# Layer 1's attention in pairs of units: two projections in one piece, end steps at even units, one fill, and a few orders in the tail

## The chip, the core and the metric

The kernel runs on one core of a Trainium2 chip. The core has five engines with a queue of instructions each: TensorE (PE, with its weight loads shown as PEld), VectorE (DVE), ScalarE (ACT), GpSimd (POOL) and SyncE (SP, which here only issues transfers). Each runs its own instructions in order and waits on semaphores for the others. The metric is the device time of one execution in microseconds (us); lower is better.

## The reference

Two transformer layers on x of shape (8, 256, 128), in fp32. Both modulate a layer norm with values from a small conditioning matrix, add attention, modulate a second layer norm, and add a mixture of experts. Layer 0 has 16 heads of 8 and eight GELU experts with a shared one, top 2. Layer 1, where nearly all of the change is, has 16 heads of 64 and 16 gated experts of width 64 with a shared one, also top 2:

```python
def _L1_attn_ref(x, w_q, w_k, w_v, w_o):
    q = jnp.einsum('bsd,hqd->bhsq', x, w_q)
    k = jnp.einsum('bsd,hqd->bhsq', x, w_k)
    v = jnp.einsum('bsd,hvd->bhsv', x, w_v)
    scores = jnp.einsum('bhsq,bhtq->bhst', q, k)
    masked = jnp.where(causal, -jnp.inf, scores)
    weights = jax.nn.softmax(masked / jnp.sqrt(jnp.float32(dq)), axis=-1)
    out = jnp.einsum('bhst,bhtv->bhsv', weights, v)
    return jnp.einsum('bsf,df->bsd', out.transpose(0, 2, 1, 3).reshape(b, s, -1), w_o)

def _L1_ffn_ref(x, ...):
    router_logits = jax.nn.sigmoid(x @ gate_w + gate_b)
    expert_values, expert_indices = jax.lax.top_k(router_logits, k=2)
    expert_values = expert_values / jnp.sum(expert_values, axis=-1, keepdims=True)
    ...   # silu(x Wg) * (x Wu) Wd of each expert, the two chosen ones weighted
    return x + _mlp(x, shared_wg, shared_wu, shared_wd) + expert_weighted

x = L0_attn_x
...   # layer 0 in the same form
h = _layernorm(x, axis=-1) * (1 + ca) + sa
x = x + ga * _L1_attn_ref(h, ...)
h = _layernorm(x, axis=-1) * (1 + cb) + sb
x = x + gb * _L1_ffn_ref(h, ...)
```

## The kernel before, in words

The kernel does layer 0's attention first, then layer 0's experts in tiles of 128 rows gathered by expert, then a loop over layer 1's attention, then a tail with layer 1's experts. Every engine's instructions are laid out in the order in which the program emits them; there is no planner.

**The loop.** Layer 1's attention has 32 units n (N, L2040): batch b = n // 4, and four heads each (u = n % 4). A unit consists of scores (`scores1`, L1666: 16 matmuls, Exp on ACT, the causal mask on POOL, L822), the projections of q and k (`project_qk1`, L1639) and of v (`project_v1`, L1651), and the values with the sums of the weights (`values1`, L1687). The result of q goes from PSUM to SBUF on DVE (L1649), those of k and v on ACT. The projections run two units ahead: in unit n the program emits scores(n), q and k of n + 2, values(n − 1), v of n + 2. Besides these there are three tables of steps hung on units: `at_head` (behind a given head's mask in the scores), `at` (behind q and k, "early") and `at_end`. Into them go the rest of layer 0 and what prepares layer 1's experts:

- the gathers (L1063, POOL) and sums (`combine`) of layer 0's expert outputs for a later batch, and the layer norm (`first_norm`: measure, normalise, modulate);
- when a batch is through, its reciprocals (`reciprocals1`, L1712, with two transfers rd and rb on SP's queue and `judge`, L817 and L818, on DVE), the four products with rb (`normalise1`, L1729), the output projection (`finish1`, L1745);
- the second layer norm of a span of batches (`norm1`), and its route (`route1`, L1790), a generator that is advanced a step at a time by `go`: logits, the sigmoid, the top two, weights, ranks (`place_steps`, L903), and then indirect scatters of the tokens into xs (L935, POOL), four for each batch;
- `clear` (L889), two fills of xs with zeros at the first units of batches 2 and 3; scatters wait for both.

**PSUM.** The tag "p" (`ps_ln`) has two buffers of one bank each, used in turn by q, k and v projections, the output projection y, transposes, logits and ranks. "s" has two buffers of two banks, for scores and the gated hidden layers; "o" and "sum" have one buffer each.

**The tail.** Ten tiles of four expert blocks (turn1, hidden1, project_tiles) run between the last norms, the routes of batches 6 and 7 (go6, go7) and the table steps (`tables`, L1017 to L1036) that find for each token where its expert's rows went. Then POOL issues 24 indirect gathers (`gather1`, L1063) with a small memset ahead of each (`apart_on_gpsimd`, L1407), which fetch the expert outputs of batches 0 to 5. Beside them run the shared expert (`shared_hidden`, `shared_project`) and, for batches 6 and 7, all 16 experts densely (`dense_hidden`, L1945), weighted by rows of gates (`gate_rows`, L1919). `combine1`, `dense_project` and `ffn1_add` end the kernel.

Of the kernel before, what the change touches and what calls it, by code (L numbers as in the profile page):

```python
# [16 lines left out]
P = 128  # L17
# [540 lines left out]
def fast_path(ctx: ExitStack, tc: tile.TileContext, i: dict, out: bass.AP, bad: bass.AP):  # L558
# [302 lines left out]
    class Sorted:  # L861


        def __init__(self, pool, tag, ne, nt, nd):
            self.pool, self.tag, self.ne, self.nt, self.nd = pool, tag, ne, nt, nd
            self.cap = cap = nt * P
            self.placed = 0
            self.fills, self.scatters = [], []
            f32 = lambda shape, name: pool.tile(shape, F32, name=f"{name}{tag}")
            self.s12 = f32([P, nt, 2, ne], "s12")  # L870
            self.slot = f32([P, nt, 2], "slot")
            self.region = f32([P, ne], "region")

            self.seen = pool.tile([P, nt + 1, ne], BF16, name=f"seen{tag}")
            self.yidx = pool.tile([P, nt, 2], I32, name=f"yidx{tag}")
            self.rowi = pool.tile([P, nd], I32, name=f"rowi{tag}")
            self.widx = pool.tile([P, nd], I32, name=f"widx{tag}")
            self.xs = dram.tile([ne * cap, P], F32, name=f"xs{tag}")
            self.ys = dram.tile([(ne + nd) * P, P], F32, name=f"ys{tag}")
            nc.gpsimd.tensor_scalar(self.region, num[:, :ne], float(cap), 0.0, ALU.mult, ALU.add)  # L880
            nc.gpsimd.memset(self.seen[:, 0, :], 0.0)
            self.marks = [pool.tile([P, 7, ne], BF16, name=f"marks{tag}{n}") for n in range(E1 // ne)]
            for t in self.marks:
                nc.gpsimd.memset(t[:, 0:3, :], 0.0)
# [1 line left out]
        def tmp(self, shape, name, dt=F32, bufs=2):  # L886
            return self.pool.tile(shape, dt, tag=name, bufs=bufs, name=f"{name}{self.tag}_{self.n}")

        def clear(self, zero, part=0, parts=1):  # L889
            m = zero.shape[1]  # L890
            n = self.ne * self.cap // m // parts
            rows = self.xs.rearrange("(p a) c -> p (a c)", p=P).rearrange("p (n m) -> p n m", m=m)
            self.fills.append(
                nc.sync.dma_start(
                    out=rows[:, bass.ts(part, n), :], in_=zero.unsqueeze(1).to_broadcast([P, n, m])
                ).ins
            )

        def place(self, *args):
            for _ in self.place_steps(*args):  # L900
# [39 lines left out]
        def apart(self, ins):  # L940


            group = f"scatters{self.tag}"
            if self.scatters:
                tc.declare_no_dep(ins, group=group, reason="different rows")
                for fill in self.fills:
                    tc.add_manual_dep(ins, fill.name, WAIT, reason="rows are cleared first")
            tc.add_to_no_dep_group(group, ins)
            self.scatters.append(ins)

# [105 lines left out]
                in_offset=bass.IndirectOffsetOnAxis(ap=self.widx[:, d : d + 1], axis=0),  # L1056
            )

        def gather(self, yg, j, between=lambda: None):

            for k in range(2):
                between()
                nc.gpsimd.indirect_dma_start(  # L1063
                    out=yg[:, k, :], out_offset=None, in_=self.ys[:, :],
                    in_offset=bass.IndirectOffsetOnAxis(ap=self.yidx[:, j, k : k + 1], axis=0),
                )
# [400 lines left out]
    at_end(18, first_gates)  # L1467
    at_end(20, first_gates)
    norm6, norm7 = norm0(SPANS0[4]), norm0(SPANS0[5])
    at_end(21, lambda: turn_gates0(0))  # L1470
    at_end(22, lambda: turn_gates0(1))
    at_end(23, norm6[0], lambda: ways[SPANS0[3]]())

    project0(0)
    project_v0(0)
# [314 lines left out]
    def route1(bs):  # L1790


        nt = 2 * bs[1]
        t = bass.ds(2 * bs[0], nt)
        name = f"1_{bs[0]}"
        shape = [P, nt, E1]
        lg = ps_ln(shape, f"lg{name}")
        for j in range(nt):
            c = bass.ts(2 * (bs[0] % 2) + j, P)
            nc.tensor.matmul(out=lg[:, j, :], lhsT=h[bs[0] // 2][:, c], rhs=w1["gate_w"], start=True, stop=True)  # L1800
        p = lp.tile(shape, F32, tag="pr", name=f"p{name}")
        nc.vector.tensor_tensor(p, lg, gate_b.unsqueeze(1).to_broadcast(shape), ALU.add)
        if bs[0] < B - 2:
            nc.scalar.activation(p, p, AF.Exp, scale=-1.0)
        else:
            nc.gpsimd.tensor_tensor(p, one_by_e.unsqueeze(1).to_broadcast(shape), p, ALU.pow)
        yield

        nc.vector.tensor_scalar(p, p, 1.0, None, ALU.add)
        nc.vector.reciprocal(p, p)  # L1810
        sparse = bs[0] < 2 * LAST
        part = bass.ds(2 * (bs[0] % 2), nt)
        s = z1.s12[:, t] if sparse else last12[:, part]
        g = g12_1[:, t]
        yield from top2_steps(lp, p, s, g, name)
        yield
        red = lp.tile([P, nt, 1], F32, tag="red", name=f"red{name}")
        nc.vector.tensor_tensor(red, g[:, :, 0:1], g[:, :, 1:2], ALU.add)
        nc.vector.reciprocal(red, red)
        nc.vector.tensor_tensor(g, g, red.to_broadcast([P, nt, 2]), ALU.mult)  # L1820
        if sparse:
            yield
            yield from z1.place_steps(2 * bs[0], nt, lambda: tokens1[bs], ps_ln)
        else:
            nc.vector.tensor_tensor(s, s, g.unsqueeze(3).to_broadcast([P, nt, 2, E1]), ALU.mult)
            nc.vector.tensor_tensor(gates1[:, part], s[:, :, 0, :], s[:, :, 1, :], ALU.add)
# [91 lines left out]

    def gate_rows(k):  # L1919

        gT_ps = pp.tile([E1, 2, P], F32, tag="s", name=f"gT1_{k}")
        for j in range(2):
            nc.tensor.transpose(gT_ps[:, j, :], gates1[:, 2 * k + j, :], ident)
        gT = lp.tile([E1, 2, P], F32, tag="yg", bufs=3, name=f"gTs1_{k}")
# [80 lines left out]
    def gather1(j):  # L2005
        k, n = divmod(j, 3)
        if n == 0:
            sums["yg", k] = lp.tile([P, 3, 2, P], F32, tag="pt", bufs=4, name=f"yg1_{k}")
        z1.gather(sums["yg", k][:, n], j, apart_on_gpsimd)

    def weigh1(w):

# [16 lines left out]
    def flag():  # L2029
# [1 line left out]
        whole = small.tile([P, 1], F32, tag="whole", bufs=1, name="whole")  # L2031
        nc.vector.tensor_reduce(whole, good, AX.X, ALU.min)
        yield
        cnt = pp.tile([1, 1], F32, tag="s", name="good_cnt")
        nc.tensor.matmul(out=cnt, lhsT=whole, rhs=nums[:, 1:2], start=True, stop=True)
        nc.vector.tensor_scalar(bad, cnt, most[0:1, :], 1.0, ALU.is_lt, ALU.mult)

# [21 lines left out]
    at(1, normalise)  # L2059
    at_end(1, modulate)  # L2060
    for j in range(2):
        at_head(0, 1 + 2 * j, lambda j=j: gather(2, j))
        at_head(1, 1 + 2 * j, lambda j=j: gather(3, j))
    at_end(1, lambda: combine(2))
    at_end(2, lambda: combine(3))
    for w in range(1, NW):
        n = 8 * w
        if w > 1:
            for k in range(4):
                at_head(n - 13 + k, 3, lambda w=w, k=k: gather(2 * w + k // 2, k % 2))  # L2070
            at_end(n - 9, lambda w=w: combine(2 * w))
            at_end(n - 8, lambda w=w: combine(2 * w + 1))
        measure, normalise, modulate = first_norm(w)
        n -= 7 if w > 1 else 6
        at_end(n, measure)
        at(n + 1, normalise)
        at_end(n + 1, modulate)
    for b in range(B - 1):
        n = 4 * b + 6 if b < B - 2 else N - 1
        at(n, *[lambda b=b, u=u: normalise1(b, u) for u in range(4)])  # L2080
        at_end(n, lambda b=b: finish1(b))
    for bs in ((0, 2), (2, 2), (4, 1), (5, 1)):
        n = 4 * sum(bs) + 2
        measure, normalise, modulate, tokens, add = norm1(bs)
        go = one(route1(bs))
        at_end(n, measure)
        at(n + 1, normalise)
        at_end(n + 1, modulate, tokens)
        at(n + 2, go)
        at_end(n + 2, go, go, go, go)  # L2090
        if bs[0] < 5:
            at(n + 4, go)
        else:
            at_end(n + 3, go)
        for k in range(4 * bs[1]):
            if bs[0] < 5:
                at_head(n + 5 + k // 2, 1 + 2 * (k % 2), go)
            else:
                at_head(n + 4, k, go)
        if bs[0] < 5:  # L2100
            at_end(n + 7, add)
    tables = one(z1.tables_steps(ps_ln, True))
    at_end(29, tables, lambda: fetch_weights1(4), lambda: fetch_weights1(5))
    at_end(30, *[lambda m=m: fetch_rows1(m) for m in range(4)], *[lambda m=m: find_rows1(m) for m in range(4, NQ)],
          lambda: fetch_weights1(6))

    for n in range(N):
        b, u = divmod(n, 4)
        scores1(b, u, behind.pop(n, {}))
        if n == 0:  # L2110
            nc.gpsimd.memset(sel, 0.0)
            nc.gpsimd.affine_select(
                out=sel, in_=sel, compare_op=ALU.not_equal, fill=1.0, base=0,
                pattern=[[-8, 4], [-32, 2], [-64, 2], [0, D1]], channel_multiplier=1,
            )
        if n + 2 < N:
            project_qk1(*divmod(n + 2, 4))
        for step in early.pop(n, ()):
            step()
        if n:  # L2120
            values1(*divmod(n - 1, 4))
        if n + 2 < N:
            project_v1(*divmod(n + 2, 4))
        if u == 0 and b:
            reciprocals1(b - 1)
            if b in (2, 3):
                z1.clear(zero1, b - 2, 2)
        for step in ends.pop(n, ()):
            step()


    norms = [norm1((b, 1)) for b in (B - 2, B - 1)]
# [13 lines left out]
    fetch_weights1(8)  # L2146
    hidden1(2)
    turn1(4)
    for _ in range(3):
        tables()  # L2150
    hidden1(3)
    norms[0][0]()
    project_tiles(2)
    hidden1(4)
    turn1(5)
    norms[0][1]()
# [4 lines left out]
    project_tiles(4)  # L2161
    spread_last((2, 3))
    hidden1(5)
    go6()
    finish1(B - 1)
    turn1(7)
# [34 lines left out]
    judge(st1["r", B - 1])  # L2201
    judged = flag()
    next(judged)
    shared_project(2)
    weigh1(2)
    dense_hidden(0)
    gate_rows(1)
    dense_hidden(1)
    dense_hidden(2)
    next(judged, None)  # L2210
    dense_hidden(3)
    dense_gate(0)
    dense_hidden(4)
# [125 lines left out]
```

## Time and profile before

| what | us |
|---|---|
| median of 14 runs (lowest, highest) | 608.98 (603.65, 613.98) |
| the profiled execution | 610.83 |
| its span | 609.0 |
| layer 1's attention loop, 240.20 to 491.00 | 250.80 |
| its PE busy time | 243.14 |
| routed tiles, 491 to 540 | 49 |
| 24 gathers issued, 540 to 575 | 35 |
| end, 575 to 609 | 34 |

Times in the views are microseconds from the span's start. A busy share is the part of the span in which an engine was at work; "<-" behind a group names what ended the idle time before it, "remote" a signal whose sender the profile does not resolve. The chain is followed back from the last instruction, and "issue" in it is time in which the engine waited for nothing that the profile shows. The granted clock is the part of TensorE's full speed that it was given. Unit 12 starts at 337.95 in the trace, unit 13 at 344.68; a unit without anything besides its own work takes 6.73.

### The profile page before, as it was taken

To read this page: it belongs to the slowest core of one execution; us is meant where nothing else is said; L and a number is where in the kernel's file an instruction comes from. 1 tells how busy PE (TensorE), PEld (TensorE's weight loads), DVE (VectorE), ACT (ScalarE), POOL (GpSimd) and SP (SyncE) were. 2 spreads that over 40 slices of the span, in tenths; PEclk is the share of its full clock that TensorE was granted. 3 is DMA by queue.
4 is the path that set the end of the run, shared out by engine and by line. 5 is a ranking of instruction groups with operands and counts; after the bars stand their busy time and mean duration, and the time that the engine had idled before them with its cause. 6 is when DMAs were issued, how large, how long until landed. Compare 5 with 4: busy or idle time off the path is not lost.

```text
span 609.0 us, 12026 instructions
## 1 busy us (share of the span) xinstructions
PE 543.8 (89%) x4499; PEld 385.3 (63%) x4499; DVE 325.3 (53%) x988; ACT 262.7 (43%) x492; POOL 272.8 (45%) x425
## 2 busy tenths in 40 slices
PE   5999998989999998999999998999989898960694
PEld 4355553468999986667667675767667576830264
DVE  4258885556322224764465646565574957660153
ACT  3677774244555533553345333443525421250110
POOL 5324676474444123854124508331654530788300
PEclk9999998799999999999999999999989998996687
DMA  8699100315999614104086593012030366552401
GB/s 273 252 398 407 38 20 30 126 41 171 318 353 351 215 40 156 32 18 93 1 258 236 131 380 93 13 26 47 19 86 14 86 199 171 155 132 56 97 19 56
DMA packets 53582, 85.40 MB, mean 140 GB/s; under 512 B 6668, under 2 KB 32780, under 8 KB 52364
## 3 DMA queue, kind: packets, MB, share of 16 engines
q1 hardware_dynamic: 45324, 60.50, 31.2%
q0 software_dynamic: 8048, 23.67, 11.9%
q8 instruction: 37, 0.61, 0.4%
q10 hardware_dynamic: 144, 0.39, 0.2%
q14 instruction: 29, 0.24, 0.1%
HBM read 53.46 MB, written 31.07 MB: 139 GB/s over the span
## 4 chain that ended last, share of the span: by engine, by line
PE 68%; DVE 11%; DMA 6%; issue 6%; ACT 4%; POOL 3%; SPq 0%; POOLq 0%; ACTq 0%; DVEq 0%
PE sc L1676 6%; PE hp L1356 6%; PE yt L1364 6%; PE sc L1125 5%; PE o L1698 5%; PE qp L1645 5%; DMA xs<-zero 4%; PE vp L1658 4%; PE kp L1645 4%; PE y L1751 4%; PE o L1159 3%; PE gud L1948 3%; PE sum L1706 3%; PE qk L1089 2%; PE sc L1137 1%
## 5 line engine op out<-in xcount | busy, mean ns | idle before, releaser
L822 POOL TENSOR_SCALAR_AFFINE_SELECT pt<-pt 128x256 f32<-128x256 f32 (+1 forms) x144 | 67.5, 496 | 146.0 <-ACT pt L1679 111.4
L1063 POOL DMA_INDIRECT yg<-ys,yidx x56 | 54.2, 968 | 32.8 <-DMA ys<-ysb 20.5
L1679 ACT ACTIVATE pt<-sc 128x768 f32<-128x768 f32 x64 | 48.4, 808 | 26.1 <-PE sc L1676 25.7
L1141 ACT ACTIVATE pt<-sc 128x1024 f32<-128x1024 f32 x48 | 46.7, 1026 | 26.0 <-PE sc L1125 14.7
L1676 PEld LDWEIGHTS sc<-q,k 64*128 64x128 f32 x512 | 41.6, 187 | 18.8 <-issue 13.9
L1698 PE MATMUL o<-pt,v 128*64 128x256 f32 (+1 forms) x512 | 50.4, 337 | 2.9 <-POOL pt L822 1.8
L1676 PE MATMUL sc<-q,k 64*128 64x256 f32 (+1 forms) x512 | 50.5, 337 | 0.0
L1358 ACT ACTIVATE hst<-hp,wt 128x128 f32<-128x128 f32 x136 | 38.8, 368 | 25.8 <-ACT hst L1358 24.2
L1661 ACT COPY v<-vp 128x512 f32<-128x512 f32 x32 | 18.7, 585 | 70.5 <-PE vp L1658 70.5
L1698 PEld LDWEIGHTS o<-pt,v 128*64 128x64 f32 x512 | 32.8, 139 | 20.8 <-POOL pt L822 7.9
L1054 POOL DMA_INDIRECT wt<-in_wpk_dram,widx x31 | 29.5, 950 | 33.8 <-PE xT L1347 27.9
L1649 DVE COPY q<-qp 128x512 f32<-128x512 f32 x32 | 22.0, 688 | 36.4 <-PE qp L1645 36.3
L1645 PE MATMUL qp<-h,wq 128*128 128x256 f32 x128 | 36.0, 404 | 3.6 <-DVE q L1649 2.3
L1369 DVE COPY ysb<-yt 128x128 f32<-128x128 f32 x39 | 11.4, 292 | 49.8 <-PE yt L1364 49.8
L935 POOL DMA_INDIRECT xs<-ht0b,idx x32 | 31.9, 996 | 11.0 <-issue 8.0
L1125 PE MATMUL sc<-qm,k 32*128 32x512 f32 x192 | 35.0, 722 | 1.6 <-ACT pt L1141 1.0
L1658 PE MATMUL vp<-wv,h 128*128 128x512 f32 x64 | 36.0, 645 | 0.0
L1356 PE MATMUL hp<-xTs,wt 128*128 128x128 f32 x272 | 35.9, 275 | 0.0
L1364 PE MATMUL yt<-wt,hst 128*128 128x128 f32 x272 | 35.8, 275 | 0.0
L1645 PE MATMUL kp<-h,wk 128*128 128x256 f32 x128 | 33.6, 386 | 0.0
L1649 ACT COPY k<-kp 128x512 f32<-128x512 f32 x32 | 18.8, 587 | 33.5 <-PE kp L1645 33.5
L1356 PEld LDWEIGHTS hp<-xTs,wt 128*128 128x128 f32 x272 | 33.0, 192 | 0.0
(306 smaller groups left out, 1095.1 us busy)
## 6 DMA issues: line engine op xcount, KB each, us to landing
xs<-zero SPq DMA_DIRECT2D x2, 6144.0 KB
xs<-zero SPq DMA_DIRECT2D x1, 8192.0 KB
rb<-rd SPq DMA_DIRECT2D x14, 512.0 KB
mdb<-mrd SPq DMA_DIRECT2D x2, 2048.0 KB
xg<-xs SPq DMA_DIRECT2D x63, 64.0 KB
wt<-in_wpk_dram SPq DMA_DIRECT2D x24, 128.0 KB
wst<-in_wpk_dram SPq DMA_DIRECT2D x5, 514.0 KB
ys<-ysb SPq DMA_DIRECT2D x10, 256.0 KB
```

The lines of the kernel that those rows point to most:

```text
L822: nc.gpsimd.affine_select(out=pt, in_=pt, compare_op=ALU.is_ge, fill=0.0, base=0, pattern=[[0, pt.shape[1]], [1, P]], channel_multiplier=-1,)
L1063: nc.gpsimd.indirect_dma_start(out=yg[:, k, :], out_offset=None, in_=self.ys[:, :], in_offset=bass.IndirectOffsetOnAxis(ap=self.yidx[:, j, ...
L1125: nc.tensor.matmul(out=sc[:, n, :].rearrange("p (a q) -> p a q", q=rhs.shape[2]), lhsT=k[r, cols], rhs=rhs, start=True, stop=u < 2,)
L1141: nc.scalar.activation(pt[:, bass.ts(half, 2), :], sc, AF.Exp)
L1356: nc.tensor.matmul(out=hp[:, c, :], lhsT=wt[:, bass.ts(c, P)], rhs=xT, start=True, stop=True)
L1364: nc.tensor.matmul(out=y, lhsT=hs[:, c, :], rhs=wt[:, bass.ds(WF + c * P, P)], start=(c == 0), stop=(c == FC - 1))
L1645: nc.tensor.matmul(out=ps_[:, n, :], lhsT=w1[f"w{what}1"][:, bass.ts(2 * u + n, P)], rhs=hb, start=True, stop=True)
L1649: copy(st1[what, b, u], ps_)
L1658: nc.tensor.matmul(out=vp, lhsT=hb[:, bass.ts(j, P)], rhs=w1["wv1"][:, bass.ts(half, 512)], start=True, stop=True)
L1676: nc.tensor.matmul(out=sc[:, n, cols], lhsT=k[r, m, bass.ts(kb, P)], rhs=q[r, m, qs], start=True, stop=True)
L1679: nc.scalar.activation(pt, sc[:, :, 0:384], AF.Exp, scale=1.0 / math.sqrt(D1))
L1698: nc.tensor.matmul(out=o[bass.ts(n, D1), m, qs], lhsT=v[:, kb, bass.ts(4 * (u % 2) + 2 * m + n, D1)], rhs=pts[m][:, n, cols], start=(kb == ...
```

## The change

The loop now runs over pairs. For an even n it emits scores(n), values(n − 1), the early steps of n, q, k and v of n + 2, the reciprocals and the fill, the end steps of n, q, k and v of n + 3, the early steps of n + 1, scores(n + 1), values(n), the end steps of n + 1. Odd units thus have no projections between their scores and their values. Gathers and scatters are hung behind head 3 of even units, four at a time, with a memset ahead of each scatter. Several steps move by a unit: the norm's measure, normalise and modulate, the products with rb and the output projection, `add`. The fill is one transfer at batch 2. In the tail the three table steps are spread, batch 7's route takes Exp on ACT as the earlier ones do, the memsets between the gathers are gone, gT and the flag's count take "p" banks instead of "s", and the shared projection, `weigh1(2)` and the flag change places with dense hidden layers. In layer 0 a step of the gates moves by one unit.

```diff
-        def clear(self, zero, part=0, parts=1):
+        def clear(self, zero):
             m = zero.shape[1]
...
-                for fill in self.fills:
-                    tc.add_manual_dep(ins, fill.name, WAIT, reason="rows are cleared first")
+                tc.add_manual_dep(ins, self.fill.name, WAIT, reason="rows are cleared first")
...
-        def gather(self, yg, j, between=lambda: None):
+        def gather(self, yg, j):
 
             for k in range(2):
-                between()
...
-    at_end(21, lambda: turn_gates0(0))
-    at_end(22, lambda: turn_gates0(1))
-    at_end(23, norm6[0], lambda: ways[SPANS0[3]]())
+    at_end(22, lambda: turn_gates0(0))
+    at_end(23, norm6[0], lambda: turn_gates0(1), lambda: ways[SPANS0[3]]())
...
-        if bs[0] < B - 2:
+        if bs[0] != B - 2:
             nc.scalar.activation(p, p, AF.Exp, scale=-1.0)
...
-        gT_ps = pp.tile([E1, 2, P], F32, tag="s", name=f"gT1_{k}")
+        gT_ps = ps_ln([E1, 2, P], f"gT1_{k}")
...
-        cnt = pp.tile([1, 1], F32, tag="s", name="good_cnt")
+        cnt = ps_ln([1, 1], "good_cnt")
...
     for j in range(2):
-        at_head(0, 1 + 2 * j, lambda j=j: gather(2, j))
-        at_head(1, 1 + 2 * j, lambda j=j: gather(3, j))
+        at_head(0, 3, lambda j=j: gather(2, j))
+        at_head(2, 3, lambda j=j: gather(3, j))
     at_end(1, lambda: combine(2))
-    at_end(2, lambda: combine(3))
+    at_end(3, lambda: combine(3))
     for w in range(1, NW):
         n = 8 * w
         if w > 1:
             for k in range(4):
-                at_head(n - 13 + k, 3, lambda w=w, k=k: gather(2 * w + k // 2, k % 2))
+                at_head(n - 12 + k // 2 * 2, 3, lambda w=w, k=k: gather(2 * w + k // 2, k % 2))
...
-        n -= 7 if w > 1 else 6
+        n -= 7 if w > 1 else 5
...
-    for b in range(B - 1):
-        n = 4 * b + 6 if b < B - 2 else N - 1
-        at(n, *[lambda b=b, u=u: normalise1(b, u) for u in range(4)])
-        at_end(n, lambda b=b: finish1(b))
+    for b in range(B - 2):
+        n = 4 * b + 6
+        steps = [lambda b=b, u=u: normalise1(b, u) for u in range(4)]
+        at(n, steps[0])
+        at_end(n, *steps[1:3])
+        at(n + 1, steps[3], lambda b=b: finish1(b))
+    at(N - 1, *[lambda u=u: normalise1(B - 2, u) for u in range(4)])
+    at_end(N - 1, lambda: finish1(B - 2))
     for bs in ((0, 2), (2, 2), (4, 1), (5, 1)):
         n = 4 * sum(bs) + 2
...
-        at_end(n, measure)
-        at(n + 1, normalise)
-        at_end(n + 1, modulate, tokens)
-        at(n + 2, go)
-        at_end(n + 2, go, go, go, go)
+        at(n + 1, measure)
+        at_end(n + 1, normalise)
+        at(n + 2, modulate, tokens)
+        at_end(n + 2, go, go, go, go, go)
...
         for k in range(4 * bs[1]):
-            if bs[0] < 5:
-                at_head(n + 5 + k // 2, 1 + 2 * (k % 2), go)
-            else:
-                at_head(n + 4, k, go)
+            m = n + 6 + k // 4 * 2 if bs[0] < 5 else n + 4
+            at_head(m, 3, lambda go=go: scatter(go, 1))
         if bs[0] < 5:
-            at_end(n + 7, add)
+            at_end(n + 4, add)
...
-    for n in range(N):
+    def project1(n):
+        if n < N:
+            project_qk1(*divmod(n, 4))
+            project_v1(*divmod(n, 4))
+
+    def run(steps):
+        for step in steps:
+            step()
+
+    for n in range(0, N, 2):
         b, u = divmod(n, 4)
         scores1(b, u, behind.pop(n, {}))
...
-        if n + 2 < N:
-            project_qk1(*divmod(n + 2, 4))
-        for step in early.pop(n, ()):
-            step()
-        if n:
-            values1(*divmod(n - 1, 4))
-        if n + 2 < N:
-            project_v1(*divmod(n + 2, 4))
+        run(early.pop(n, ()))
+        project1(n + 2)
         if u == 0 and b:
             reciprocals1(b - 1)
-            if b in (2, 3):
-                z1.clear(zero1, b - 2, 2)
-        for step in ends.pop(n, ()):
-            step()
+            if b == 2:
+                z1.clear(zero1)
+        run(ends.pop(n, ()))
+        project1(n + 3)
+        run(early.pop(n + 1, ()))
+        scores1(b, u + 1, behind.pop(n + 1, {}))
+        values1(b, u)
+        run(ends.pop(n + 1, ()))
...
-    for _ in range(3):
-        tables()
+    tables()
     hidden1(3)
     norms[0][0]()
     project_tiles(2)
+    tables()
     hidden1(4)
...
     hidden1(5)
+    tables()
     go6()
...
-    shared_project(2)
-    weigh1(2)
     dense_hidden(0)
     gate_rows(1)
+    weigh1(2)
+    next(judged, None)
     dense_hidden(1)
+    shared_project(2)
     dense_hidden(2)
-    next(judged, None)
     dense_hidden(3)
```

More of the change, by code (lines that the diff above doesn't have):

```diff
@@ L867, in __init__ @@
             self.placed = 0
-            self.fills, self.scatters = [], []
+            self.scatters = []
             f32 = lambda shape, name: pool.tile(shape, F32, name=f"{name}{tag}")
@@ L887, in tmp @@
             return self.pool.tile(shape, dt, tag=name, bufs=bufs, name=f"{name}{self.tag}_{self.n}")
-        def clear(self, zero, part=0, parts=1):
+        def clear(self, zero):
             m = zero.shape[1]
[L891 to L897, printed above, removed]
+            self.fill = nc.sync.dma_start(
+                out=self.xs.rearrange("(p a) c -> p (a c)", p=P).rearrange("p (n m) -> p n m", m=m),
+                in_=zero.unsqueeze(1).to_broadcast([P, self.ne * self.cap // m, m]),
+            ).ins
         def place(self, *args):
@@ L2008, in gather1 @@
             sums["yg", k] = lp.tile([P, 3, 2, P], F32, tag="pt", bufs=4, name=f"yg1_{k}")
-        z1.gather(sums["yg", k][:, n], j, apart_on_gpsimd)
+        z1.gather(sums["yg", k][:, n], j)
     def weigh1(w):
@@ L2105, in fast_path @@
           lambda: fetch_weights1(6))
-    for n in range(N):
+    def project1(n):
[6 more added lines that the diff above has]
+    for n in range(0, N, 2):
         b, u = divmod(n, 4)
         scores1(b, u, behind.pop(n, {}))
-        if n == 0:
+        if n:
+            values1(*divmod(n - 1, 4))
+        else:
             nc.gpsimd.memset(sel, 0.0)
```

## The prediction

> **What bounds the kernel now.** I read the page's busy line and chain first, then the windows table by stage, then in each stage what ended PE's idle time.
>
> ```profile
> PE 543.8 (89%) x4499; PEld 385.3 (63%) x4499; DVE 325.3 (53%) x988; ACT 262.7 (43%) x492; POOL 272.8 (45%) x425
> PE 68%; DVE 11%; DMA 6%; issue 6%; ACT 4%; POOL 3%; SPq 0%; POOLq 0%; ACTq 0%; DVEq 0%
> ```
>
> PE is the bound, but the share is a mean over stages. The windows table (columns: busy us and count of each engine, granted clock, DMA share, GB/s) has layer 1's attention loop, the routed tiles, the 35 us in which the 24 gathers are issued, and the end:
>
> ```profile
> 240.20:491.00 250.80, 243.14 (x2077) 170.38 (x2077) 149.97 (x373) 108.35 (x154) 114.73 (x193) 0.99 0.33 99
> 491.00:540.00 49.00, 43.49 (x412) 33.08 (x410) 30.03 (x92) 16.41 (x39) 19.71 (x16) 0.97 0.57 161
> 540.00:575.00 35.00, 10.97 (x46) 5.00 (x46) 6.77 (x25) 4.22 (x12) 25.52 (x47) 0.71 0.35 87
> 575.00:609.00 34.00, 24.52 (x134) 17.53 (x134) 14.86 (x26) 3.08 (x6) 0.00 (x0) 0.80 0.19 53
> ```
>
> In the loop PE idles only 250.80 − 243.14 = 7.7 us; the one stretch at half clock there (449.0 to 452.3, clock 0.50) adds some 1.7. So 9.4 us is all that any order of the loop can win. The third row is another matter: 24 us idle. The chain and the timeline show it:
>
> ```profile
> 545.85 19.63 issue
> 565.48 0.70 DVE a L1943
> ```
>
> ```profile
> 544.80 1.12 PE L1948 MATMUL gud<-h,wg 128*128 128x512 f32 x2
> 545.76 1.02 PE L1948 MATMUL gud<-h,wu 128*128 128x512 f32 x2
> 564.85 0.60 ACT L1942 ACTIVATE a<-gud 128x512 f32<-128x512 f32 x1 [22.23 <-remote]
> 568.99 0.95 POOL L1063 DMA_INDIRECT yg<-ys,yidx  x1 [0.19 <-issue]
> ```
>
> By the records gud is ready at 546.78 and ACT starts at 564.85, near the end of POOL's gathers (540.02 to 569.94). What holds it, the profile does not say.
>
> **The change part by part.**
>
> *Two projections in one piece.* The loop's DVE work around unit 12 shows what matters:
>
> ```profile
> 338.12 1.76 DVE L1714 RECIPROCAL r<-sum 128x256 f32<-128x256 f32 x1 [1.21 <-PE vp L1658]
> 339.91 0.65 DVE L817 SCALAR_TENSOR_TENSOR good<-r,good 128x256 f32<-128x256 f32 x1
> 341.02 0.39 DVE L1809 TENSOR_SCALAR p<-p 128x64 f32<-128x64 f32 x1
> 345.79 0.18 DVE L917 TENSOR_TENSOR seen<-seen,mall 128x16 bf16<-128x16 bf16 x1
> 345.88 0.68 DVE L1649 COPY q<-qp 128x512 f32<-128x512 f32 x1
> 346.62 0.70 PE L1645 MATMUL qp<-h,wq 128*128 128x256 f32 x2 [0.36 <-DVE q L1649]
> ```
>
> From reciprocal to route's end DVE works 345.88 − 338.12 = 7.76 us without a pause, the q copy stands behind it, and yet PE waits 0.36: between two users of that "p" bank lie scores, values and v-projection. In the new order q(n+2), k, v, then unit n's end steps, then q(n+3), k, v follow each other on PE, all in two "p" banks, and the end steps stand on DVE between the copies of q(n+2) and q(n+3). v(n+3) needs the bank of q(n+3), and scores(n+1) and values(n) are queued behind it on PE. At n = 12 DVE needs, from the end of q(14)'s matmuls, 0.68 + 7.76 + 0.23 (adding the bias) + 0.24 (Exp on ACT) + 0.68 = 9.6 us; PE has k, v, q, k (0.96 + 1.05 + 0.96 + 0.96, by the starts in unit 12: q 339.46, k 340.42, values 341.38, v 343.62, scores 344.68) and the logits, about 0.3: 4.2. Stall 5.4, so 10.8 for n = 12 and 20. At n = 24 and 28 the route has half the tokens: reciprocal and judging 2.92, bias and Exp 0.45, the 128x32 steps 3.8 by the later route at 539.55 to 544.52, two copies 1.36: 8.5 − 4.2 = 4.3, so 8.6. At n = 8 and 16 reciprocal, judging and a combine of 2.2 (L1384 to L1388): 6.5 − 3.9 = 2.6, so 5.2. At n = 10 and 18 a normalise or two of the four products with rb stand there: 1.85 each, 3.7. n = 0 and 4: 0.9 and 0.8. Sum 30.0, of which nothing is covered, since PE has no slack to take it from. The bounds: below, half of it, 15, if what DVE does early (the chain may start while PE still runs v) is undercounted; above, 36, by the chain at 439.47 to 447.07, which took 7.6 for 128x32 tiles while POOL worked beside it (one step 1.97 instead of 0.19).
>
> Against it stand the 9.4 us that the old order loses; most have the same causes in the old places (2.0 before unit 26's q, the half clock after it), so I take all of it off: net +21.
>
> *The clock.* The half-clock stretch of 3.3 us came in the trace after an idle of 1.96 and cost 1.7. Four stalls above 4 us can bring 0 to 6.8; I take one, 1.7, since before's other pauses brought none. The Trainium skill (TensorE: Matmul & The Clock Gate, Part 1) says that about 3.4 us of idleness sets the half clock for a window of the same length; by it all four stalls pay and the sum would be 5 us higher. The row's stretch agrees in length, though its idle time was shorter than the rule asks.
>
> *One fill in place of two.* Before, the second fill, issued at 342.83, ended at 366.4 (23.6 us), and the first scatter waited 8.6 us for it, PE then 1.8 for a mask behind that scatter. One fill at n = 8 (307.7) of twice the bytes ends by two times 23.6 at about 355, and scatters now start at unit 16: the wait goes (counted in the 9.4). SP's rd and rb of batch 2 stand behind this fill; needed at unit 14, at about 350 to 358: 0 to 3 us, I take 1. With this the loop is +22.
>
> *Gathers and scatters four at a time at even units.* Four times the period of 1.25 is 5.0 us on POOL behind head 3's mask, and the next scores come only after two projections and values (about 8.3 us): nothing, up to 1 us if a mask is late. The memsets added to the scatters and taken from the last gathers cost nothing: 0.94 + 0.19 + 0.12 with one, 0.95 + 0.30 without. In layer 0 a gate step moves by one unit: nothing, PE is fed there by the other units.
>
> *The tail.* Three table steps in one piece on DVE lie on the chain from 504.29 to 508.19 (3.9 us); spread behind hidden1, I take 2.5 off (0 to 3.9). Batch 7's route takes Exp on ACT in place of POOL's power (534.10, 5.42 us). The gathers stood behind it on POOL, first at 540.02; they now wait for the last store of ys, issued by 536.68: 0 to 2.5 earlier, I take 1.3. ACT pays two table loads of 1.28 (as at 497.93) while it would wait for matmuls. The Trainium skill (ScalarE: Activation LUTs, What ACT_TABLE_LOAD costs) counts about 2.7 us for each change of set, a load and a drain; in the trace the next activation starts 0.01 us after the load, and by the rule the sum would be 2.8 us higher at most. gT and the count go from the "s" banks to "p", so gud0 and gud1 can both run before ACT takes the first; gud1 (566.23 to 570.00, at half clock) leaves the path if its signal comes with gud0's: 0 to 4, I take 2. Tail −5.8.
>
> **Sum.** 610.83 (the profiled execution; its span is 609.0) + 22 + 1.7 − 5.8 = 628.7. It lies 1.85 above the median 608.98, so 626.9; I say 627. The loop should grow from 250.8 to about 274.
>
> **Rivals.**
>
> *The 19.63 us close.* If what delays gud's signal goes with the shared banks or the memsets, the dense part runs under the gathers: the tail gives 2.5 + 1.3 + 19.6 + 4 = 27.4, the end 610.83 + 23.7 − 27.4 = 607.1, less 1.85: 605.3, faster. Not slower than 0.5% from the point where 15 of the 23.6 come back. For: gT in an "s" bank sits between gud0 and gud1. Against: by the records gud0's matmuls were not waiting for a bank, and the signals come at the gathers' end, which stay.
>
> *Half the stalls.* DVE's chain begins earlier than I count; loop 15 − 9.4 + 1 = 6.6, no clock price, tail −5.8: 611.6 − 1.85 = 609.8, no change. For: before's PE ran with waits of 0.36 at the same chain. Against: the instructions' order on DVE and the two banks.
>
> *Longer stalls.* Stretched chains (+6) and all four clock prices (+5): 638. For: the 1.97 us step. Against: POOL has fewer masks beside the chain when PE stands still.
>
> **How the numbers follow.** Forecast 0.50, closing 0.20, half 0.15, longer 0.15. About 0.5% (606 to 612) is what a measurement of this kernel can tell from no change. The forecast's own range is 618 to 633, all slower; closing gives 0.15 faster, 0.05 same; half gives 0.03 faster, 0.07 same, 0.05 slower; longer 0.15 slower. That makes 0.18, 0.12 and 0.70; the chance of faster takes 0.03 from the middle, a band too narrow for 0.12: 0.21, 0.09, 0.70. The range reaches from inside the closing case, 604, to 636.
>
> **What would show it.** In the changed profile PE should wait for DVE's q copy (the line of vp or of qp, k) in units 12, 20, 24 and 28, 4 to 6 us each, with more half-clock slices around 350 to 490; no scatter waits for the fill; no table step stands in one piece around 504; POOL has no power; ACT's first a from gud still starts within 5 us of the last gather. The prediction is wrong if the v-projection finds its bank free, which the first view would show, or if the idle stretch behind gud is gone, which the windows of the tail would show.

## The result, and the profile after

The changed kernel is slower, by far less than forecast: 612.55 us median of 10 runs (610.54 to 615.02) against 607.89 of 47 runs for the kernel before (599.11 to 614.55). The ratio is 1.012, with a 95% interval of 1.0094 to 1.0147. Ratios in this text leave out executions more than 1.5% above the fastest of their kernel, here 21 of the 47 and none of the changed kernel's (in `tail_only` below, one of 691.12 us at a clock of 0.747), so this one is above the 1.008 of the two medians. The profiled execution took 615.44, its span is 613.3; I had forecast 627.

The page of the changed kernel (busy times, and the chain's shares):

```profile
PE 541.5 (88%) x4499; PEld 384.8 (63%) x4499; DVE 328.9 (54%) x988; ACT 266.7 (43%) x495; POOL 266.2 (43%) x424
PE 69%; DVE 9%; DMA 5%; another core or an unknown queue 5%; ACT 5%; issue 3%; POOL 1%; SPq 1%; ACTq 0%; POOLq 0%; DVEq 0%
```

Its windows table, by the stages of before (columns: busy us and count of each engine, granted clock, DMA share, GB/s):

```profile
239.10:497.45 258.35, 239.02 (x2074) 168.15 (x2074) 150.85 (x373) 109.33 (x154) 115.92 (x216) 0.99 0.32 96
497.45:547.00 49.55, 44.77 (x409) 34.21 (x409) 32.12 (x98) 18.40 (x41) 14.45 (x15) 0.90 0.57 161
547.00:582.00 35.00, 15.20 (x60) 6.80 (x56) 6.50 (x20) 5.57 (x14) 22.79 (x24) 0.74 0.50 106
582.00:613.30 31.30, 22.25 (x128) 16.58 (x128) 14.13 (x24) 2.56 (x5) 0.00 (x0) 0.83 0.10 36
```

PE's idle time in the loop went from 7.7 to 19.3 us. Measured from the first scores of unit 0 to the first scores of unit 31, which is free of the choice of an end, the loop went from 244.08 to 251.35 us, so 7.3 longer; from there to the end, 124.7 went to 122.8, 1.9 shorter; and the loop began 1.1 earlier. Together 4.3, the difference of the two spans. A second trace of the kernel before (`before_again`, below) has 242.02 in this loop and a span of 606.8, so such differences between two traces are good to some 2 us.

The stall that the forecast rests on is not there. Unit 12 in the timeline of the changed kernel:

```profile
336.88 1.75 DVE L1708 RECIPROCAL r<-sum 128x256 f32<-128x256 f32 x1
340.15 1.03 PE L1639 MATMUL kp<-h,wk 128*128 128x256 f32 x4
341.27 0.59 ACT L1643 COPY k<-kp 128x512 f32<-128x512 f32 x1 [1.30 <-PE kp L1639]
341.91 1.12 PE L1652 MATMUL vp<-wv,h 128*128 128x512 f32 x2 [0.73 <-ACT k L1643]
347.50 0.69 DVE L1643 COPY q<-qp 128x512 f32<-128x512 f32 x1
```

The q copy comes even later than I had counted, 10.6 us after the reciprocal began. But the v projection that follows k ran 5.6 us before that copy and had waited 0.73 for ACT's copy of k, not for DVE. It had been given k's bank.

Where the loop did lose time is units 14 and 15: 24.07 us from the scores of 14 to those of 16, where before had 18.10. The chain and then the timeline of the changed kernel there:

```profile
338.65 7.60 DMA rd<-r
...
346.84 6.29 DMA rb<-rd
353.12 0.43 issue
353.55 0.69 DVE ou L1725
```

```profile
353.55 0.69 DVE L1725 TENSOR_TENSOR ou<-ou,rb 128x512 f32<-128x512 f32 x1 [2.37 <-DMA rb<-rd]
354.43 1.13 PE L1639 MATMUL kp<-h,wk 128*128 128x256 f32 x4 [1.99 <-issue]
356.31 0.68 DVE L1643 COPY q<-qp 128x512 f32<-128x512 f32 x1
357.05 2.07 PE L1652 MATMUL vp<-wv,h 128*128 128x512 f32 x2 [1.49 <-DVE q L1643]
358.91 1.91 PE L1639 MATMUL qp<-h,wq 128*128 128x256 f32 x4
```

rd of batch 2 takes 7.6 us behind the single fill, and rb another 6.3. In the kernel before, rd of batch 2 was followed by rb 1.78 later:

```profile
339.91 0.50 SPq L1719 DMA_DIRECT2D rd<-r  x1
341.69 1.09 SPq L1722 DMA_DIRECT2D rb<-rd  x2
```

DVE then waits for rb ahead of the q copy, and PE waits behind DVE twice: k at 354.43, which the profile puts down to "issue", waits in the program for DVE's copy of the ranks, which stands behind ou; v at 357.05 waits for the q copy. From 355.6, where the second pause begins, to 362.5 the granted clock is 0.50 (q takes 1.91 instead of 1.11).

In the tail the late signals are still there, in three pieces in place of one:

```profile
554.29 0.60 ACT L1936 ACTIVATE a<-gud 128x512 f32<-128x512 f32 x1 [5.03 <-remote]
562.78 0.60 ACT L1936 ACTIVATE a<-gud 128x512 f32<-128x512 f32 x1 [5.56 <-remote]
565.11 1.02 PE L1942 MATMUL gud<-h,wu 128*128 128x512 f32 x2
575.86 0.94 POOL L1058 DMA_INDIRECT yg<-ys,yidx  x1 [0.30 <-issue]
581.08 1.09 ACT L1936 ACTIVATE a<-gud 128x512 f32<-128x512 f32 x2 [17.71 <-remote]
```

### The profile page after: what moved, and what is told of

Same layout as the page of the kernel before. It is cut to its first block, busy times and chain, and to the rows that moved or that the text cites. A ratio compares the mean times of both kernels' runs of the same rounds, so it can differ in the third digit from the quotient of the medians.

```text
span 613.3 us, 12021 instructions
## 1 busy us (share of the span) xinstructions
PE 541.5 (88%) x4499; PEld 384.8 (63%) x4499; DVE 328.9 (54%) x988; ACT 266.7 (43%) x495; POOL 266.2 (43%) x424
## 4 chain that ended last, share of the span: by engine, by line
PE 69%; DVE 9%; DMA 5%; another core or an unknown queue 5%; ACT 5%; issue 3%; POOL 1%; SPq 1%; ACTq 0%; POOLq 0%; DVEq 0%
PE sc L1670 7%; PE o L1692 6%; PE hp L1351 6%; PE yt L1359 6%; PE sc L1120 5%; PE vp L1652 5%; PE y L1745 4%; PE qp L1639 4%; PE kp L1639 3%; PE sum L1700 3%; PE o L1154 3%; PE gud L1942 2%; PE hp L1274 2%; PE qk L1084 2%
## 5 line engine op out<-in xcount | busy, mean ns | idle before, releaser
L822 POOL TENSOR_SCALAR_AFFINE_SELECT pt<-pt 128x256 f32<-128x256 f32 (+1 forms) x144 | 66.2, 492 | 165.0 <-ACT pt L1673 130.3
L1692 PE MATMUL o<-pt,v 128*64 128x256 f32 (+1 forms) x512 | 48.7, 332 | 2.7 <-DVE ou L1704 2.7
L1704 DVE COPY ou<-o 128x512 f32<-128x512 f32 x32 | 22.1, 690 | 44.6 <-PE o L1692 44.5
L1050 POOL DMA_INDIRECT wt<-in_wpk_dram,widx x31 | 29.5, 952 | 33.7 <-PE xT L1342 29.8
L1639 PE MATMUL kp<-h,wk 128*128 128x256 f32 x128 | 35.0, 396 | 3.6 <-issue 2.0
L932 POOL DMA_INDIRECT xs<-ht0b,idx x32 | 31.9, 998 | 11.7 <-issue 11.5
L1359 PEld LDWEIGHTS yt<-wt,hst 128*128 128x128 f32 x272 | 33.0, 192 | 0.0
```

Source lines behind the costliest of these rows:

```text
L822: nc.gpsimd.affine_select(out=pt, in_=pt, compare_op=ALU.is_ge, fill=0.0, base=0, pattern=[[0, pt.shape[1]], [1, P]], channel_multiplier=-1,)
L1359: nc.tensor.matmul(out=y, lhsT=hs[:, c, :], rhs=wt[:, bass.ds(WF + c * P, P)], start=(c == 0), stop=(c == FC - 1))
L1639: nc.tensor.matmul(out=ps_[:, n, :], lhsT=w1[f"w{what}1"][:, bass.ts(2 * u + n, P)], rhs=hb, start=True, stop=True)
L1692: nc.tensor.matmul(out=o[bass.ts(n, D1), m, qs], lhsT=v[:, kb, bass.ts(4 * (u % 2) + 2 * m + n, D1)], rhs=pts[m][:, n, cols], start=(kb == ...
```

## The experiments

My theory after the result had three parts. The sums over DVE were right and only the bank was wrong; the single fill is what the loop lost; and the idle stretch in the tail belongs to the gathers, so that the tail's edits could bring little. The rivals were that the DVE sums were too high, that the pairing itself costs, and that banks or code loading cause the stretch.

**Banks strictly in turn (`in_turn`).** The changed kernel, with layer 1's "p" banks given out by turns.

```diff
     def ps_ln(shape, name):
-        return pp.tile(shape, F32, tag="p", name=name)
+        if not turn:
+            return pp.tile(shape, F32, tag="p", name=name)
+        turn[0] ^= 1
+        return pp.tile(shape, F32, tag=f"p{turn[0]}", bufs=1, name=name)
```

> The changed kernel with layer 1's p banks given out strictly in turn, so that the v projection of an odd unit gets the bank of that unit's q, as the prediction took for granted. If the prediction's DVE sums were right and only the bank was not: the v projection waits for DVE's q copy 5.4 us in units 12 and 20, 4.3 in 24 and 28, 2.6 in 8 and 16, and the loop grows by about 20 us over the changed kernel's. If the sums were too high: waits below 2.5 us, the loop grows by less than 10.

It took 640.52 us (2 runs; ratio to before 1.0536, 1.0456 to 1.0616). PE's waits in its loop, and some of the v projections of its timeline:

```profile
PE vp L1658 <- DVE q L1649: 31.9, 13, 6.6
```

```profile
308.38 1.12 PE L1658 MATMUL vp<-wv,h 128*128 128x512 f32 x2 [2.35 <-DVE q L1649]
349.61 2.08 PE L1658 MATMUL vp<-wv,h 128*128 128x512 f32 x2 [6.57 <-DVE q L1649]
385.93 2.08 PE L1658 MATMUL vp<-wv,h 128*128 128x512 f32 x2 [2.53 <-DVE q L1649]
426.54 1.80 PE L1658 MATMUL vp<-wv,h 128*128 128x512 f32 x2 [4.33 <-DVE q L1649]
466.07 2.08 PE L1658 MATMUL vp<-wv,h 128*128 128x512 f32 x2 [4.62 <-DVE q L1649]
```

These are units 8, 12, 16, 20 and 24, forecast at 2.6, 5.4, 2.6, 5.4 and 4.3; unit 28 waited 5.42, where 4.3 was forecast. All these waits come to 31.9, of which 30.5 lie in the units that my sum of 30.0 names; single units differ by up to 1.2. Half clock stands behind four of those shown (2.08 and 1.80 instead of 1.12) and behind unit 28: 23.8 us of the loop in all. From scores 0 to scores 31 the loop grew by 25.8 over the changed kernel's and by 33.1 over that of before. The sum of the stalls was right, and the bank was the whole of the error in this term. It was not the only error of the forecast: with the banks as I had them, the kernel takes 13.5 us more than 627, and lies beyond the range.

**The tail's edits alone (`tail_only`).** The kernel before, with the changed tail: the spread table steps, Exp, the "p" banks, the order of the dense part, the gathers without memsets.

```diff
-        if bs[0] < B - 2:
+        if bs[0] != B - 2:
...
-        gT_ps = pp.tile([E1, 2, P], F32, tag="s", name=f"gT1_{k}")
+        gT_ps = ps_ln([E1, 2, P], f"gT1_{k}")
...
-        z1.gather(sums["yg", k][:, n], j, apart_on_gpsimd)
+        z1.gather(sums["yg", k][:, n], j)
```

> The kernel before with the tail's edits alone (spread table steps, Exp on ACT for batch 7, no memsets between the last gathers, gT and the count in the p banks, the changed order of the dense part). From the loop's last unit to the end the two traces show 117.7 us before and 115.9 after. If the tail's edits are worth what these show: 1 to 3 us faster. If my term of 5.8 was right and the loop hid it: 5 to 7 us faster, the idle stretch behind gud still ending with the gathers. If the idle stretch behind gud hung on the banks: over 20 us faster.

604.04 us against 608.61 (ratio 0.9934, 0.9897 to 0.9972), so some 4 us faster (4.6 by the medians). From scores 31 to the end three profiles of the old tail in this study take 124.7, 123.3 and 125.3 (before, `one_fill`, `before_again`), five of the new one 122.8, 121.9, 121.6, 120.6 and 119.6 (after, `tail_only`, `pairs_two_fills`, `in_turn`, `tail_again`): 3.1 less in the mean. My term of 5.8 was too large, and the low figure in the expectation, read from two traces, too low.

**One fill alone (`one_fill`).** The kernel before, with the fill as one transfer.

```diff
-            if b in (2, 3):
-                z1.clear(zero1, b - 2, 2)
+            if b == 2:
+                z1.clear(zero1)
```

> The kernel before with the fill of xs as one transfer at batch 2, nothing else. If the fill holds the transfers rd and rb of batch 2 behind it (in the changed kernel rd takes 7.6 us and rb 6.3): PE idles 3 to 5 us around unit 14, part of it followed by half clock, the 1.8 us wait of unit 16 goes, and the kernel is 3 to 5 us slower. If my price of 1 us for it was right: 1 us faster.

610.17 us against 608.61 (ratio 1.0041, 1.0004 to 1.0078): slower, by 2.5 by the ratio and 1.6 by the medians, which is little more than can be told from no change, and less than the 3 to 5 expected. The stall is where it was expected, on a smaller scale:

```profile
353.36 2.50 DVE L1727 TENSOR_TENSOR ou<-ou,rb 128x512 f32<-128x512 f32 x4 [5.05 <-DMA rb<-rd]
354.20 4.21 PE L1747 MATMUL y<-wo,ou 128*128 128x128 f32 x32 [2.23 <-DVE ou L1727]
```

DVE waits 5.05 for rb, PE 2.23. Units 14 and 15 take 20.56 (before: 18.10), units 16 and 17 take 13.45 (before: 15.86), since no scatter waits for a second fill. In the loop of this one profile the two cancel, so only the timing says slower, and that weakly. What the fill costs thus depends on the order around it: the old order has values and a v projection between the wait and PE's need of it.

**The changed kernel with two fills (`pairs_two_fills`).**

```diff
-            if b == 2:
-                z1.clear(zero1)
+            if b in (2, 3):
+                z1.clear(zero1, b - 2, 2)
```

> The changed kernel with the two half fills of before. If the single fill is what lengthens units 14 and 15 from 18.1 to 24.1 us: they come back to 18 or 19, unit 16 may wait 1 or 2 us for the second fill, and the kernel is 4 to 6 us faster than the changed one, within 0.3% of before. If the pairing itself costs: it stays 4 us or more slower than before.

608.64 us (ratio 1.0025, 0.9991 to 1.006), no difference from before that can be told. Units 14 and 15 come back from 24.07 to 18.54, and the loop from 251.35 to 246.15: the single fill cost the changed kernel 5.2 us in these two profiles. Units 16 and 17 show no wait for the second fill, since scatters start at the end of that stretch.

What remains is the pairing. `tail_only` has the same tail and fills with the old order: 242.49 in the same measure, 3.7 less, and 0.9934 against 1.0025 in the timings (medians 604.04 and 608.64). The old order's loop took 242.02 to 244.36 in the eight traces of it on chips of this speed, so by the profiles the pairing costs 1.8 to 4.1. PE's waits in the loop of `pairs_two_fills` (us in total, times, longest) suggest where most of it goes:

```profile
PE vp L1656 <- ACT k L1647: 5.0, 7, 0.7
PE vp L1656 <- issue: 2.8, 5, 0.7
PE o L1696 <- DVE ou L1708: 2.7, 2, 2.1
PE vp L1656 <- DVE q L1647: 1.4, 2, 1.1
```

With k and v side by side, v waits 0.73 for ACT to drain k's bank in each of the eight even units whose second v was given that bank (three of these waits stand under "issue"); the old order does not have these waits and has the 2.0 us of unit 26 instead. No run removes these waits alone, so that they are the price of the pairing is argued and not shown.

**Without the tail's gathers (`no_gathers`, `eight_gathers`), and with spaced ones (`spaced`).** The kernel with the tail's edits alone, in which the 24 gathers are left out, cut to 8, or set apart by a memset of 128x512.

```diff
-        z1.gather(sums["yg", k][:, n], j)          # no_gathers
+            nc.vector.memset(sums["yg", k], 0.0)
...
-        z1.gather(sums["yg", k][:, n], j)          # eight_gathers
+        if j < 4:
+            z1.gather(sums["yg", k][:, n], j)
+        else:
+            nc.vector.memset(sums["yg", k][:, n], 0.0)
...
-        z1.gather(sums["yg", k][:, n], j)          # spaced
+        z1.gather(sums["yg", k][:, n], j, lambda: nc.gpsimd.memset(room, 0.0))
```

> The kernel with the tail's edits alone, without the 24 gathers of the tail: yg is filled with zeros by VectorE, so the routed part of batches 0 to 5 is left out. If the gathers hold TensorE's signals back: ACT takes gud within 1 us of its matmuls, the idle stretch of some 15 to 20 us is gone and the kernel ends 20 to 27 us earlier. If the stretch has another cause (instruction loading, a bank): it stays above 10 us.

> The same with the first 8 of the 24 gathers, the rest of yg zeros, so most of the routed part of batches 0 to 5 is left out. If signals are held back as long as gathers are being issued or in flight: the delay ends with the eighth gather, 10 to 14 us after the first, and the tail is 12 to 20 us shorter. If the delay builds up only after many gathers: no signal is late by more than 3 us.

> The kernel with the tail's edits alone, with a memset of 128x512 (0.52 us in the trace) ahead of each of the 24 gathers: their period grows from 1.25 to about 1.8 us and the last starts 12 us later. If the rate of the gathers is what holds the signals back: the signals of gud come within 1 or 2 us and the kernel is faster by 5 to 15 us. If any gather in flight does it: the idle stretch grows with the gathers, and the kernel is 10 to 13 us slower.

570.46, 571.05 and 578.76 us. In none of them does ACT wait longer than 3.4 us for gud, and spaced gathers are 1.8% faster than before (ratio 0.9819, 0.9768 to 0.987). But on the chip that ran these the kernel before took 589.84, some 3% less than elsewhere, and the unspaced kernel had not run there. Before, the tail's edits, spaced gathers and none were therefore compared on one chip.

> The kernel before once more, for its trace on the chip that runs the three below (the chip of the gather runs showed a mean clock of 0.99 and had the kernel before at 589.84 us). If the idle stretch behind gud belongs to the program: 15 to 20 us again. If it depends on the chip: it differs from 19.6 us, with the same instructions.

> The tail's edits alone once more, on one chip with the three others. If the edits are worth the same on any chip: 0.3 to 1% faster than before; its idle stretches behind gud0 to gud3 as long in sum as before's one.

> The spaced gathers once more. If spacing is what lets the signals come in time: no stretch behind gud above 3.4 us on this chip either while the unspaced kernel of the same call has some, and 1 to 2.5% faster than before. If the earlier chip was the cause: the stretch is back, and it is 12 us slower than the unspaced one.

> The run without the tail's 24 gathers (zeros in their place, so the routed part of batches 0 to 5 is left out), on the same chip as the unspaced kernel. If gathers hold the signals: no stretch behind gud, where the unspaced kernel has one. If something else does: both have it.

On that chip: before 608.89 (13 runs, and 608.48 for the run with the trace), the tail's edits 603.33 (ratio 0.9955, 0.9909 to 1.0001), spaced gathers 588.55 (0.9711, 0.9607 to 0.9815), no gathers 575.82. What ACT waited for before the activation of gud, in the tails of before, of the tail's edits, of spaced gathers and of none (us in total, times, longest):

```profile
ACT a L1942 <- remote: 29.8, 1, 29.8
```

```profile
ACT a L1941 <- remote: 28.8, 3, 17.7
```

```profile
ACT a L1943 <- PE gud L1949: 14.9, 7, 3.4
```

```profile
ACT a L1941 <- PE gud L1947: 15.2, 7, 3.6
```

The waits alone do not say how late a signal is. The timeline of the spaced kernel has ACT start 0.04 us after the record of its matmuls ends:

```profile
540.59 1.02 PE L1949 MATMUL gud<-h,wu 128*128 128x512 f32 x2
541.65 0.60 ACT L1943 ACTIVATE a<-gud 128x512 f32<-128x512 f32 x1 [2.83 <-PE gud L1949]
```

Without gathers it is 0.04 as well; in `before_again` the first activation starts 25.6 us after that record, in `tail_again` the first three 2.6, 8.2 and 21.9.

Spacing does what leaving the gathers out does: the late signals are gone, and the waits left are those of PE's own pace. The rate matters, not the gathers as such: from scores 31 to the end the spaced kernel takes 103.7 us and the unspaced one 119.6, although the spaced gathers occupy POOL longer.

**A smaller pause (`half_space`).** The same with a memset of 128x256.

```diff
-    room = lp.tile([P, 512], F32, bufs=1, name="room")
+    room = lp.tile([P, 256], F32, bufs=1, name="room")
```

> The tail's edits with a memset of 128x256 (0.32 us in the trace) ahead of each gather: the period falls from 1.66 to about 1.46 us, the last gather starts 4.6 us earlier than with 128x512. With the memset of 128x1 that the kernel before has (0.12 us, period 1.25) the signals were late. If any period above 1.25 is enough: no stretch behind gud above 3.4 us, and 0.3 to 0.8% faster than the wide spacing, so 3 to 3.7% faster than before. If it takes more pause: a stretch of 3 to 15 us is back and the gain of the wide spacing (2.9%) is partly lost.

583.86 us against 608.35 (ratio 0.9576, 0.9502 to 0.9651). It beats both kernels of this case, by 4.2% the one before, more than the 3 to 3.7% expected (on another chip than the spaced run). The timeline of its gathers, what ACT waited for, and the last wait of PE:

```profile
541.56 0.96 POOL L1064 DMA_INDIRECT yg<-ys,yidx  x1 [0.17 <-issue]
543.01 0.95 POOL L1064 DMA_INDIRECT yg<-ys,yidx  x1 [0.16 <-issue]
...
577.26 0.79 PE L2027 MATMUL of<-yg,dg 128*128 128x128 f32 x2 [2.31 <-DMA yg<-ys,yidx]
```

```profile
ACT a L1943 <- PE gud L1949: 6.4, 3, 2.9
ACT a L1943 <- issue: 5.6, 3, 3.4
```

A period of 1.45 us is enough where 1.25 was not. The kernel before has a memset between its gathers too, but one of 128x1, with which the period stays 1.25. What bounds the end now is the gathers themselves: the last matmuls wait for their landing.

## Why the prediction was wrong, point by point

- **The bank: the step that failed.** "v(n+3) needs the bank of q(n+3)" took for granted that two buffers are handed out by turns. The program's pool gave v of unit 15 the bank of k. No profile was needed to see it: the changed program's instruction list, in which no time stands, names the engine whose signal each instruction waits for, and I had built the sum without reading that line:

```
L1639 Matmult kp1_3_3_3866<-h1_112,wk1_154 128x256 [waits DVE_49]
L1652 Matmult vp1_3_3_3871<-wv1_156,h1_112 128x512 [waits Activation_49]
```

  In all eight even units to which I gave 1.85 us or more (8, 10, 12, 16, 18, 20, 24 and 28) the second v waits for ACT alone. In units 14, 22 and 26 it waits for DVE, at no cost; the 1.49 of unit 14 was lost by the first v there, that of unit 16, which has the bank of its q. In the kernel before, too, the banks are not "used in turn", as I described them above: its built program gives v of unit 15 the bank of k. `in_turn` shows the counterfactual: 31.9 us of stalls where the sum was 30.0. In that sum the logits were given 0.3 us, while their group takes 0.99 from its start to the next group's (333.66 to 334.65 in the trace of before); against it, two steps of DVE's chain in unit 12 of `in_turn` took 1.50 and 1.29 instead of 0.22. So single terms of it came out partly by luck. The rival "half the stalls" put the doubt in the DVE sum, which in total was right, and named the two banks as evidence against itself.
- **Net of the loop, +21 for the pairing:** 3.7 by `pairs_two_fills` against `tail_only`, 1.8 to 4.1 against all traces of the old order. The waits that did come are those for ACT's copy of k, 0.73 each, which I had not counted at all.
- **The single fill, priced at 1 us (0 to 3):** 5.2 in the changed kernel. The mechanism was named, SP's rd and rb behind the fill. The fill itself ended earlier than I had worked out, its last packet at 345.7 and not at about 355; but rd landed only then (346.25), rb took its 6.3 us after it, and the order multiplied the delay: rb's late arrival blocks DVE ahead of a q copy that PE needs at once, and half clock goes with it. In the old order the same fill lengthens units 14 and 15 by 2.5. The Trainium skill (DMA: Bandwidth & Descriptors, Queues, rings and completion order) says that each DMA engine takes the descriptors of a ring in their order; rd's 7.60 us behind the fill agrees with that.
- **The wait for the second fill goes:** right where it was tried alone, 15.86 to 13.45 in units 16 and 17 of `one_fill`. I had put it in the loop's 9.4, of which the traces show this, the 2.0 of unit 26 and the half clock behind that pause to be gone; the new order's own waits took their place.
- **The clock, one window of 1.7:** too small. The changed kernel has half clock for 6.8 us in units 14 and 15, around the pauses of 1.99 and 1.49, twice the 3.4 of before; PE works in 5.45 of them, so that they cost about 2.7 by the reckoning that gave 1.7. With the stalls that I had forecast, in `in_turn`, it is 23.8 us in five stretches, PE at work in 20.7 of them, about 10.3 by the same reckoning, where I had put 6.8 as the most.
- **The tail, −5.8:** −1.9 between the two profiles, −3.1 over eight of them, and the timing of `tail_only` says −4. gud1 did run ahead of ACT, but its signal came 8 us late, so the 2 us that I gave it were not there. The gathers did not start earlier: 55.7 us after the scores of unit 31 before, 56.6 in the changed kernel, where I had taken 1.3 off. The power's 5.4 us on POOL for batch 7 gave way to two table loads of 1.28, as counted (batch 6's power stays, at 525.60). The load at 539.02 began 0.01 us after the activation ahead of it and was followed by its own at 540.32, 0.02 us after its end, so the drain of about 1.4 us that the Trainium skill counts with each load (ScalarE: Activation LUTs, What ACT_TABLE_LOAD costs) does not show here.
- **The idle stretch stays as long as the gathers are issued at this pace:** right, though in three pieces, and the reason for it, which I had called open, is their pace. The rival "the 19.63 us close" was rightly ranked for this change, since nothing in it slows the gathers.
- **Direction and range.** Slower was right; that the time lies inside the range is luck, because the range reached down for other reasons. The rival "half the stalls" (609.8) is nearest by its number, also by luck: DVE's chain did not begin earlier than counted. 18 us were forecast, and the two medians differ by 4.7, the ratio of 1.012 makes 7.3.

## What to carry to other kernels

Where the order of buffers decides a stall, read in the built program which engine's signal the waiting instruction names, before any sum is made; a pool need not hand out its buffers by turns. A large transfer costs what is queued behind it on the same queue, and how much that is depends on whether the waiting engine stands ahead of something the bound engine needs next. When an engine's results seem to arrive long after its work is recorded, look at what another engine issues in an unbroken row at that time, and set it apart before anything else is rearranged.

## What the runs showed of the hardware that I had not expected

- While POOL issued indirect gathers with a period of 1.25 us, ACT took the results of TensorE's matmuls late: it waited 5.0, 5.6 and 17.7 us in the changed kernel and 29.8 in one piece in `before_again`, and started 2.7, 8.4, 17.9 and 25.6 us after the records of the matmuls end. Signals from ACT to DVE came at once (ACT's a at 554.29 ends at 554.89, DVE follows at 554.92). With periods of 1.45 and 1.66 us ACT started 0.04 us after the record. Through which path is not shown: whether it is the signal or the matmuls themselves that are held, these traces can't tell, since they model the ends of matmuls.
- The late starts go by the gathers' clock: in `after`, `tail_only`, `tail_again` and `pairs_two_fills` the first comes 7.28 to 7.33 us after the first gather, and the third 5.2 to 5.3 us after the start of the last one.
- Eight gathers at the close period did not do it on the fast chip: ACT started at most 0.14 us after the record, twice while they were being issued. The unspaced kernel was not traced there, so whether the number of gathers or the chip makes this difference is open.
- A pause of 1.96 us in unit 26 was followed by a half-clock stretch in some executions of the same order and not in others: units 26 and 27 took 20.96 us in before and `tail_again`, 19.43 in `tail_only` and `one_fill`, and 19.44 in `before_again`, which is the same program as before. Pauses of 2.23 us (`one_fill`, unit 14) and 2.35 (`in_turn`, unit 8) were not followed by one. So the pause that brings it can be well below the 3.4 us that the Trainium skill gives as the idle window (TensorE: Matmul & The Clock Gate, Part 1).
- One chip ran the kernel before in 589.84 us, where others took 608; its mean granted clock was 0.970 to 0.980 there and 0.951 to 0.969 elsewhere. The same kernel without gathers differs between this chip and another by 5.4 us, with spaced gathers by 9.8, the kernel before by 19. So the idle stretch was probably shorter there, which no trace shows.
